# Output step of a gated Toeplitz layer: second half sorted by tile shape, the remaining channels in four quarters of the array

## The chip, the cores and the metric
One core of a Trainium2 chip runs the whole program. Times are device microseconds for one launch; a kernel's time is the median of its runs. The engines are TensorE (PE; its weight loads are listed as PEld), VectorE (DVE), ScalarE (ACT) and GpSimd (POOL). SyncE (SP) only issues transfers, and POOL issues some of them too.

## The reference
Four layers act one after the other on an image tensor `x` of 8 samples, 56 x 56 positions, 192 channels, all in fp32. Each is `x = x + layer(groupnorm(x))`. Layers 0 and 1 have this form:

```python
p = silu(x @ p_w.T + p_b)              # 192 -> 576 channels
q = silu(x @ q_w.T + q_b)
v = silu(x @ v_w.T + v_b)
o1 = toeplitz(q * v, a1)               # along the rows of the image
o2 = toeplitz(q * v, a2)               # along its columns
out = (p * (o1 + o2)) @ o_w.T + o_b    # 576 -> 192 channels
```

Layer 2 is a 7 x 7 depthwise convolution with an MLP, layer 3 a windowed attention. The change touches layers 0 and 1 only.

## The kernel before
**Stages of layers 0 and 1.** Samples are worked on in pairs (j and j + 4), and pairs in two groups of two (`j0` = 0 and 2). For each layer and group there are three stages. `tno_qv` (Q) computes `q * v` and writes it to DRAM. `tno_toeplitz` (TZ) multiplies it by Toeplitz matrices along rows and columns and writes the sum `o1 + o2` to the DRAM array `L_sum`, called `o` in the code. `tno_out` (O) reads the sum, computes `p`, gates, multiplies by `o_w` and writes the layer's result `y`.

**Weaving.** A planner (`weave`) runs one lane of stages and lets another generator emit a step whenever its share of the planned time is due. In order: TZ of layer 0, group 0 beside Q of group 1; TZ of layer 0, group 1 beside O of layer 0, group 0 (below: pass A) and Q of layer 1, group 0; TZ of layer 1, group 0 beside O of layer 0, group 1 (pass B) and Q of layer 1, group 1; TZ of layer 1, group 1 beside O of layer 1, group 0 (pass C); last, the convolution's first half beside O of layer 1, group 1 (pass D). PE, ACT, DVE and POOL keep the order in which the code emits their instructions during the Toeplitz stages. When a lane stage is 90% done, the rest of the Toeplitz steps is emitted and the first loads of the next O follow. So each pass's sums are complete before O loads them.

**Toeplitz stage.** Its 9 blocks hold 64 channels each. L405 multiplies in tiles of 56 rows x 32 columns of the array, 8 of them side by side. ACT copies (L412), DVE transposes (L423, L425), POOL adds the column direction (L427), and `store` issues four POOL transfers (L437) for each half of a block. `store` puts 128 channels into a *part* of `o`: parts 0 to 3 are the first 512 channels of the pair's first sample, 4 to 7 those of the second, and part 8 holds the remaining 64 channels of both samples, one on partitions 0 to 63, the other on 64 to 127 (`row + b // 2 * 64`). The ninth block is the one that goes to part 8.

**Output stage.** A tile is 224 positions of a pair; 14 tiles make a pair and 28 a pass. 576 channels are 4 x 128 + 64, and 192 are 128 + 64, so each product has pieces of four shapes. The moving operand always has 224 columns. `inner` computes `p` for the first 512 channels (L530: full array; L539: 64 rows x 128 columns, two at once), ACT applies Silu (L549) and POOL, in pass D DVE, multiplies into the sums (L556). `outer` works on two tiles at once: `now`, for which it makes the 64 remaining channels of `p` (`rem`; L565: 128 x 64, L567: 64 x 64), and `before`, the tile before it, whose output product it makes: 128 output channels from the remaining 64 inputs (L572: 64 x 128) and from the 512 (L575: full array), and 64 output channels (`po2`) from the 512 (L578: 128 x 64) and from the remaining 64 (L580: 64 x 64). `rem` and `po2` share one PSUM tile `P` of two banks with the 128-channel result: `po2` lies in the first bank, `rem` in the second. Then come Silu of `rem` (L584), its gate (L585), the residual (L588, L591), the store of `y` (L122, on POOL) and the statistics (L594). The sums' tile, three buffers deep, also takes the gated values and then `y`, so that a load of sums (L502, on SP) waits for a store of `y` from three tiles earlier.

Of the kernel before, what the change touches and what calls it, by code (L numbers as in the profile page):

```python
# [26 lines left out]
B, H, W, C = 8, 56, 56, 192  # L27
T = H * W
HALF = [slice(0, 64), slice(64, 128)]
TT = 448  # L30
NT = T // TT
D1 = 576
# [11 lines left out]
class Net:  # L44
# [320 lines left out]
    def tno_toeplitz(self, j0, mats, qv, o):  # L365

        nc, p = self.nc, self.tz
        PR = H // 2  # L370

        def load(n):
            blk, d = divmod(n, 2)
            q = p.tile([128, H, 128], F32, name="q", bufs=2)
            if d == 0:

                for half in range(2):
                    of = qv[2 * blk + half, :T].rearrange("(h w) e -> w h e", w=W)
                    nc.sync.dma_start(q[64 * half : 64 * half + W], of)  # L379
            else:  # L380
                of = qv[2 * blk : 2 * blk + 2].rearrange("n (h w) e -> (n h) (w e)", w=W)
                nc.sync.dma_start(q.rearrange("p i e -> p (i e)"), of)
            return q

        def matrices(n):

            blk, d = divmod(n, 2)
            row = 32 * self.TW
            at = mats[d].offset + 2 * blk * self.TG * row
            for k in range(4):  # L390
                of = bass.AP(mats[d].tensor, at + k, [[row, 2 * self.TG], [1, row]])
                nc.sync.dma_start(self.tms[n % 2][k:128:4], of)  # L392

        def along(n, q, ot, g):


            d, tm = n % 2, self.tms[n % 2]
            pt = self.bank2()
            for hf in range(2):
                for j in range(4):  # L400
                    c = 4 * g + j
                    at = c * self.TW + (28 if d else 24) * hf
                    for r in range(2):
                        rows = slice(64 * r, 64 * r + 56)
                        nc.tensor.matmul(  # L405
                            pt[32 * j : 32 * j + 32, r, hf * 224 : (hf + 1) * 224],
                            tm[rows, at : at + 32],
                            q[rows, :, 4 * c : 4 * c + 4],
                            start=True,
                            stop=True,  # L410
                        )
            nc.scalar.copy(  # L412
                view(ot, 4 * (g % 4), [[16, 2], [32, 112], [1, 4]]),
                view(pt, 0, [[512, 2], [4, 112], [1, 4]]),
            )

        def turned(d, ot, s, hf):


            of = ot[:, hf * 56 * 32 : (hf + 1) * 56 * 32]  # L420
            if d == 0:
                to = view(s, 55 - 24 * hf, [[W, 56], [-1, 32]])
                nc.vector.transpose(to, of.rearrange("p (i k) -> p i k", k=32))  # L423
            else:
                nc.vector.transpose(of, of)  # L425
                to = view(s, (55 - 28 * hf) * W, [[-W, 28], [1, 56]])
                nc.gpsimd.tensor_add(to, to, view(of, 0, [[1, 28], [32, 56]]))  # L427

        def store(blk, s, half):
            for b in range(4):  # L430
                part, row = divmod(blk * DC + 32 * half, 128)
                if part < 4:
                    part += b // 2 * 4
                else:
                    part, row = 8, row + b // 2 * 64
                to = o[j0 + b % 2, part, row : row + 32, :]
                nc.gpsimd.dma_start(to, s[b : 128 : 4])  # L437

        NS = 2 * (D1 // DC)
        loaded = []  # L440
        for n in range(2):
            loaded.append(load(n))
            matrices(n)
        yield 8.0

        work = []

        def behind():


            if work:
                d, ot, s, half, hf, blk = work.pop(0)
                turned(d, ot, s, hf)
                if d and hf:
                    store(blk, s, half)

        for n in range(NS):
            blk, d = divmod(n, 2)
            q = loaded.pop(0)
            if d == 0:  # L460
                ss = [p.tile([128, T], F32, name="s", bufs=2) for half in range(2)]
            for g in range(8):
                if g % 4 == 0:
                    ot = p.tile([128, 2 * 56 * 32], F32, name="ot", bufs=2)
                along(n, q, ot, g)
                if g % 4 == 3:
                    work += [(d, ot, ss[g // 4], g // 4, hf, blk) for hf in range(2)]
                if g % 2:
                    if g == 7 and n + 2 < NS:
                        loaded.append(load(n + 2))  # L470
                        matrices(n + 2)
                    yield 3.2
                    behind()
        while work:
            behind()

    def tno_out(self, L, j0, xs, gn, o, ys, gn_next, woven):
# [3 lines left out]
        nc, p, inp = self.nc, self.tp, self.inp  # L481
        N = 224
# [5 lines left out]
        pw = wo[:, : 2 * D1].rearrange("p (k c) -> p k c", k=2)  # L488
        ow = wo[:, 2 * D1 : 2 * D1 + 5 * C].rearrange("p (k c) -> p k c", k=5)
# [15 lines left out]
        def normalize(j, x):  # L505
            xn = p.tile([128, 3, N], F32, name="t4")
            for k in range(3):
                if woven:
                    nc.scalar.activation(  # L509
                        xn[:, k, :],  # L510
                        x[:, k, :],
                        AF.Identity,
                        bias=gn[:, j, k, 1:2],
                        scale=gn[:, j, k, 0:1],
                    )
                else:
                    nc.vector.tensor_scalar(
                        xn[:, k, :], x[:, k, :], gn[:, j, k, 0:1], gn[:, j, k, 1:2], ALU.mult, ALU.add
                    )
            return xn  # L520

        mm = nc.tensor.matmul
# [35 lines left out]
        def outer(now, before, after=None):  # L558

            P = self.bank2()  # L560
            po2, rem = P[:, 0, 256 : 256 + N], P[:, 1, 256 : 256 + N]
            if now:
                xn, s = now[5], now[3]
                for b in range(2):
                    mm(rem[HALF[b]], pw[:, 0, 512:D1], xn[:, b], start=True, stop=False)  # L565
                for b in range(2):
                    mm(rem[HALF[b]], pw[HALF[b], 1, 512:D1], xn[HALF[b], 2], start=False, stop=not before)  # L567
            if before:
                j, t, x, g, st, _ = before
                for b in range(2):  # L570
                    fresh = b == 0 or not now
                    mm(P[:, b, :N], ow[HALF[b], 4, 0:128], g[HALF[b], 8], start=fresh, stop=False)  # L572
                for c in range(4):
                    for b in range(2):
                        mm(P[:, b, :N], ow[:, c, 0:128], g[:, 4 * b + c], start=False, stop=c == 3 and b == 1)  # L575
                for c in range(4):
                    for b in range(2):
                        mm(po2[HALF[b]], ow[:, c, 128:C], g[:, 4 * b + c], start=False, stop=False)  # L578
                for e in range(2):
                    mm(po2[HALF[e]], ow[HALF[e], 4, 128:C], g[HALF[e], 8], start=False, stop=True)  # L580
            xn = normalize(*after) if after else None
            if now:
                pg = p.tile([128, N], F32, name="t1", bufs=1)
                nc.scalar.activation(pg, rem, AF.Silu, bias=pb[:, 4:5])  # L584
                gate.tensor_mul(s[:, 8], s[:, 8], pg)  # L585
            if before:
                y = g[:, 0:3]
                nc.vector.scalar_tensor_tensor(  # L588
                    y[:, 0:2], P[:, :, :N], ob[:, 0:1], x[:, 0:2], ALU.add, ALU.add
                )  # L590
                nc.vector.scalar_tensor_tensor(y[:, 2], po2, ob[:, 1:2], x[:, 2], ALU.add, ALU.add)  # L591
                self.store_pair(ys, j, slice(t * N, (t + 1) * N), y)
                for k in range(3):
                    nc.vector.bn_stats(st[:, k, t, :], y[:, k, :])  # L594
                if t == T // N - 1:
                    self.norms.append(self.pair_gn_finish(st, gn_next, j))
            return xn

        tiles = [(j, t) for j in (j0, j0 + 1) for t in range(T // N)]
        before = None  # L600
        x2 = load_x(*tiles[0])
        s = load_s(*tiles[0])
        if woven:
            yield None
            xn = normalize(j0, x2[:, :, :N])
        yield 0.0
        if not woven:
            xn = normalize(j0, x2[:, :, :N])
# [1037 lines left out]
```

## Time and profile before

| what | value |
| --- | --- |
| median of 3 runs | 5809.6 us (5804.27 to 5814.28) |
| profiled execution | 5811.1 us, its span 5809.3 us |
| PE busy | 5361.1 us, 92% of the span |
| POOL busy | 2207.7 us, 38% |
| pass A, B, C, D (us from the span's start) | 985 to 1415, 1790 to 2260, 2610 to 3235, 3235 to 3805 |
| granted TensorE clock | 0.957 of full speed over the span |

A line of the timeline has the start in us, the length in us, the engine, the line of the code, the operation, output and input tiles, for matmuls the rows * columns of the array in use and the shape, and how many instructions were merged (x16). In brackets stands how long the engine was idle before, and what ended that. An fp32 matmul appears as two records. A length runs to the modelled end of a pipelined matmul, so that start-to-start differences are the better measure of steps on PE.

### The profile page before, as it was taken

The numbers are of one execution on the slowest core, as the hardware profiler recorded it, in microseconds if no ns is written. First come the engines' busy times: TensorE is split into PE (matmuls) and PEld (weight loads), VectorE is DVE, ScalarE is ACT, GpSimd is POOL, SyncE is SP. The second block draws the span as 40 slices with busy tenths as digits, with TensorE's granted clock in tenths as the row PEclk, the third lists the DMA queues.
The fourth block names the chain that finished last, engine by engine and source line by source line (L and its number), as shares of the span: only waits on it lengthen the run. The fifth ranks groups of instructions, "written<-read, shape, count | busy, mean of one in ns | idle before, by whom it ended". The sixth has DMA issues, their size and how long they took to land.

```text
span 5809.3 us, 144273 instructions
## 1 busy us (share of the span) xinstructions
PE 5361.1 (92%) x64672; PEld 3889.9 (67%) x64672; DVE 2365.9 (41%) x3770; ACT 2269.1 (39%) x2990; POOL 2207.7 (38%) x1528
## 2 busy tenths in 40 slices
PE   6998888999999999998898889999999999989987
PEld 3776666777777777776676678855664445666765
DVE  6444444233553333552343322422113232555555
ACT  2434444444554444454444322242324333333332
POOL 2335565565565556565567100000001002333332
PEclk9999999999999999999999899999999999999998
DMA  8559997887886887978998556634444222434442
GB/s 277 137 150 263 274 293 217 261 255 225 246 262 197 254 245 236 251 218 239 296 307 266 175 200 223 212 127 162 145 149 117 67 67 54 85 90 93 88 95 48
DMA packets 1029771, 1098.79 MB, mean 189 GB/s; under 512 B 232769, under 2 KB 966977, under 8 KB 1013729
## 3 DMA queue, kind: packets, MB, share of 16 engines
q1 hardware_dynamic: 993568, 888.57, 55.6%
q0 software_dynamic: 35584, 200.99, 9.1%
q8 instruction: 509, 8.34, 0.6%
q14 instruction: 110, 0.89, 0.0%
HBM read 725.48 MB, written 363.94 MB: 188 GB/s over the span
## 4 chain that ended last, share of the span: by engine, by line
PE 59%; SPq 9%; DMA 9%; POOL 9%; DVE 7%; issue 4%; ACT 2%; POOLq 0%; DVEq 0%; ACTq 0%
PE bank L263 12%; PE bank L955 7%; PE bank L816 5%; PE bank L1035 4%; SPq L392 4%; PE bank L530 4%; POOL s L427 4%; PE bank L405 4%; PE bank L575 3%; DMA qv<-t 3%; SPq L379 3%; PE bank L1049 3%; DMA t<-L_sum 3%; PE bank L539 2%; PE bank L578 2%
## 5 line engine op out<-in xcount | busy, mean ns | idle before, releaser
L263 PE MATMUL bank<-wq,t 128*128 128x256 f32 (+4 forms) x7680 | 1293.7, 376 | 81.4 <-DVE t L272 41.6
L263 PEld LDWEIGHTS bank<-wq,t 128*128 128x128 f32 (+2 forms) x7680 | 1009.5, 191 | 359.5 <-issue 103.5
L272 DVE TENSOR_TENSOR t<-bank,wq 128x1024 f32<-128x1024 f32 (+3 forms) x480 | 517.7, 1112 | 774.0 <-PE bank L263 554.7
L304 POOL TENSOR_TENSOR t<-t 128x1024 f32<-128x1024 f32 (+2 forms) x288 | 519.5, 1818 | 650.0 <-ACT t L301 326.7
L412 ACT COPY ot<-bank 128x896 f32<-128x896 f32 x576 | 493.3, 914 | 622.4 <-PE bank L405 361.2
L427 POOL TENSOR_TENSOR s<-s,ot 128x1568 f32<-128x1568 f32 x144 | 618.9, 4303 | 64.8 <-DVE ot L425 64.1
L405 PE MATMUL bank<-q,tm 56*32 56x224 f32 x18432 | 523.0, 362 | 83.6 <-DMA tm<-L_tab 27.5
L301 ACT ACTIVATE t<-t 128x2048 f32<-128x2048 f32 (+2 forms) x288 | 421.9, 1488 | 398.2 <-DVE t L272 394.8
L405 PEld LDWEIGHTS bank<-q,tm 56*32 56x32 f32 x18432 | 352.6, 108 | 221.2 <-issue 117.5
L556 POOL TENSOR_TENSOR t<-t,t 128x896 f32<-128x896 f32 x168 | 347.4, 2086 | 358.7 <-DMA t<-L_sum 189.5
L588 DVE SCALAR_TENSOR_TENSOR t<-bank,wo,t 128x448 f32<-128x448 f32 x112 | 76.4, 682 | 890.0 <-ACT t L584 517.1
L530 PE MATMUL bank<-t,wo 128*128 128x224 f32 x1792 | 397.1, 378 | 44.4 <-ACT t L509 22.6
L955 PE MATMUL bank<-z,w 128*128 128x448 f32 (+1 forms) x1344 | 413.6, 555 | 2.0 <-ACT h L964 2.0
L549 ACT ACTIVATE t<-bank,wo 128x448 f32<-128x448 f32 x448 | 248.5, 635 | 407.2 <-PE bank L539 379.8
L530 PEld LDWEIGHTS bank<-t,wo 128*128 128x128 f32 x1792 | 352.5, 203 | 81.4 <-issue 28.2
L575 PE MATMUL bank<-t,wo 128*128 128x224 f32 x1792 | 378.6, 365 | 0.0
L127 POOL DMA_DIRECT2D x<-x x64 | 36.8, 575 | 862.4 <-DVE x L986 832.9
L575 PEld LDWEIGHTS bank<-t,wo 128*128 128x128 f32 x1792 | 337.7, 194 | 34.0 <-issue 32.3
L816 PEld LDWEIGHTS bank<-xt,cm 113*112 113x112 f32 x3072 | 315.0, 180 | 45.0 <-issue 37.4
L423 DVE STREAM_TRANSPOSE s<-ot 128x1792 f32<-128x1792 f32 x144 | 292.6, 2034 | 109.3 <-DMA L_sum<-s 63.9
L816 PE MATMUL bank<-xt,cm 113*112 113x108 f32 (+2 forms) x3072 | 326.2, 266 | 7.7 <-ACT h L964 4.5
L955 PEld LDWEIGHTS bank<-z,w 128*128 128x128 f32 (+1 forms) x1344 | 182.2, 189 | 205.8 <-issue 197.5
(149 smaller groups left out, 7004.3 us busy)
## 6 DMA issues: line engine op xcount, KB each, us to landing
q<-qv SPq DMA_DIRECT2D x36, 3584.0 KB
q<-qv SPq DMA_DIRECT2D x72, 1568.0 KB
L_sum<-s POOLq DMA_DIRECT2D x288, 392.0 KB, 7.2
t<-L_sum SPq DMA_DIRECT2D x112, 1008.0 KB
qv<-t SPq DMA_DIRECT2D x192, 512.0 KB
cm<-in_L_cm SPq DMA_DIRECT2D x96, 896.0 KB
tm<-L_tab SPq DMA_DIRECT2D x288, 240.0 KB
x<-t POOLq DMA_DIRECT2D x112, 336.0 KB, 7.0
```

The costliest lines, as they stand in the source:

```text
L263: nc.tensor.matmul(pp[:m, b, 256 * j : 256 * j + k], x[rows, j, 2 if part else b, s : s + m], w[rows, part, c0 + c : c0 + c + k],  start=p ...
L272: nc.vector.tensor_add(z[:m, c : c + k, :], view(pp[:m], 0, [[1, k], [256, 4]]), view(bias[:m], c0 + c, [[1, k], [0, 4]]),)
L301: nc.scalar.activation(z[:m, :n, :], z[:m, :n, :], AF.Silu)
L304: nc.gpsimd.tensor_mul(prod[:m, :k], half[:, :, 0], half[:, :, 1])
L405: nc.tensor.matmul(pt[32 * j : 32 * j + 32, r, hf * 224 : (hf + 1) * 224], tm[rows, at : at + 32], q[rows, :, 4 * c : 4 * c + 4], start=Tr ...
L412: nc.scalar.copy(view(ot, 4 * (g % 4), [[16, 2], [32, 112], [1, 4]]), view(pt, 0, [[512, 2], [4, 112], [1, 4]]),)
L427: nc.gpsimd.tensor_add(to, to, view(of, 0, [[1, 28], [32, 56]]))
L530: mm(gs[c // 2][:, b, c % 2 * 256 : c % 2 * 256 + N], pw[:, 0, 128 * c : 128 * c + 128], xn[:, b], start=c % 2 == 0, stop=False,)
L556: gate.tensor_mul(to, to, pg)
L575: mm(P[:, b, :N], ow[:, c, 0:128], g[:, 4 * b + c], start=False, stop=c == 3 and b == 1)
L816: nc.tensor.matmul(pc[:, 128 * e + 4 * m0 : 128 * e + 4 * m1], cm[:113, e, k, :], xt[:, m0 - 1 + k : m1 - 1 + k, c + e, :], start=n == 0 a ...
L955: nc.tensor.matmul(phs[c][:, s, :TT], w0[rows, part, at : at + 128], z[rows, Z[2 if part else s], :], start=part == flip, stop=part != flip,)
```

## The change
In `outer`, the matmuls are put in another order. First come up to four 64 x 64 products together: the two of `rem` from the 64-row piece and the two of `po2` from the remaining 64 channels. Then come the 128 x 64 products of `rem` and `po2`, then the 64 x 128, last the full-array products.

For the four 64 x 64 products to lie in four different quarters of the array, the two samples of the remaining channels change halves on every other tile (`turn` for `now`, `back` for `before`): on odd tiles `rem` is made with the samples' partitions exchanged, and the matmuls that read them follow. The sums have to come in the same arrangement, so `store` writes part 8 in two transfers per `b`, one for the even and one for the odd tiles of 224 positions, the latter to the other half of the partitions. The normalization of the next tile (`xn`) is emitted between the matmul groups and no longer after them.

```diff
-                else:
-                    part, row = 8, row + b // 2 * 64
-                to = o[j0 + b % 2, part, row : row + 32, :]
-                nc.gpsimd.dma_start(to, s[b : 128 : 4])
+                    to = o[j0 + b % 2, part + b // 2 * 4, row : row + 32, :]
+                    nc.gpsimd.dma_start(to, s[b : 128 : 4])
+                    continue
+                for turn in range(2):
+                    at = row + 64 * (b // 2 ^ turn)
+                    to, of = (
+                        ap.rearrange("p (t k n) -> p t k n", k=2, n=224)[:, :, turn]
+                        for ap in (o[j0 + b % 2, 8, at : at + 32, :], s[b : 128 : 4])
+                    )
+                    nc.gpsimd.dma_start(to, of)
...
+            turn = now[1] % 2 if now else 0
             if now:
                 xn, s = now[5], now[3]
-                for b in range(2):
-                    mm(rem[HALF[b]], pw[:, 0, 512:D1], xn[:, b], start=True, stop=False)
-                for b in range(2):
-                    mm(rem[HALF[b]], pw[HALF[b], 1, 512:D1], xn[HALF[b], 2], start=False, stop=not before)
             if before:
                 j, t, x, g, st, _ = before
+                back = t % 2
+            for b in range(2):
+                if now:
+                    r = HALF[b ^ turn]
+                    mm(rem[r], pw[HALF[b], 1, 512:D1], xn[HALF[b], 2], start=True, stop=False)
+                if before:
+                    r = HALF[b ^ back]
+                    mm(po2[HALF[b]], ow[r, 4, 128:C], g[r, 8], start=True, stop=False)
+            if now:
                 for b in range(2):
-                    fresh = b == 0 or not now
-                    mm(P[:, b, :N], ow[HALF[b], 4, 0:128], g[HALF[b], 8], start=fresh, stop=False)
-                for c in range(4):
-                    for b in range(2):
-                        mm(P[:, b, :N], ow[:, c, 0:128], g[:, 4 * b + c], start=False, stop=c == 3 and b == 1)
+                    mm(rem[HALF[b ^ turn]], pw[:, 0, 512:D1], xn[:, b], start=False, stop=not before)
+            xn = normalize(*after) if after else None
+            if before:
                 for c in range(4):
                     for b in range(2):
                         mm(po2[HALF[b]], ow[:, c, 128:C], g[:, 4 * b + c], start=False, stop=False)
-                for e in range(2):
-                    mm(po2[HALF[e]], ow[HALF[e], 4, 128:C], g[HALF[e], 8], start=False, stop=True)
-            xn = normalize(*after) if after else None
+                for b in range(2):
+                    r = HALF[b ^ back]
+                    mm(P[:, b, :N], ow[r, 4, 0:128], g[r, 8], start=b == 1 and not now, stop=False)
+                for c in range(4):
+                    for b in range(2):
+                        mm(P[:, b, :N], ow[:, c, 0:128], g[:, 4 * b + c], start=False, stop=c == 3)
```

More of the change, by code (lines that the diff above doesn't have):

```diff
@@ L432, in store @@
                 if part < 4:
-                    part += b // 2 * 4
-                else:
-                    part, row = 8, row + b // 2 * 64
-                to = o[j0 + b % 2, part, row : row + 32, :]
-                nc.gpsimd.dma_start(to, s[b : 128 : 4])
+                    to = o[j0 + b % 2, part + b // 2 * 4, row : row + 32, :]
[8 more added lines that the diff above has]
+                    nc.gpsimd.dma_start(to, of)
         NS = 2 * (D1 // DC)
```

## The prediction
> **What bounds the kernel now.** I read the page first for the engine shares, then a table of stretches for the four passes of the output step (A to D), then the timeline of single tiles, then the waits around the stores of a Toeplitz pass.
>
> ```profile
> PE 5361.1 (92%) x64672; PEld 3889.9 (67%) x64672; DVE 2365.9 (41%) x3770; ACT 2269.1 (39%) x2990; POOL 2207.7 (38%) x1528
> ```
> ```profile
> core 0: us, PE busy (x) PEld busy (x) DVE busy (x) ACT busy (x) POOL busy (x), PEclk, DMA share, GB/s
> 985.00:1415.00 430.00, 412.86 (x4672) 313.60 (x4671) 129.35 (x185) 182.61 (x302) 250.64 (x165) 0.98 0.87 252
> 1790.00:2260.00 470.00, 451.06 (x4933) 343.19 (x4932) 146.15 (x209) 201.07 (x327) 261.82 (x172) 0.97 0.86 246
> 2610.00:3235.00 625.00, 534.34 (x7148) 405.38 (x7145) 225.38 (x245) 259.08 (x396) 391.30 (x242) 0.92 0.92 272
> 3235.00:3805.00 570.00, 536.54 (x3989) 448.45 (x3989) 186.96 (x441) 148.03 (x256) 26.79 (x40) 0.95 0.57 194
> ```
> The rows are A, B, C and D. In A and B TensorE is 96% busy, in D 94%: PE is the first limit there. In C it is 85% busy with the DMA engines at 0.92; between 2700 and 3100 us they are at 1.0. There PE is not the limit.
>
> One tile of A, TensorE alone:
> ```profile
> 1266.85 1.74 PE L405 MATMUL bank<-q,tm 56*32 56x224 f32 x64
> 1268.53 0.60 PE L565 MATMUL bank<-t,wo 128*64 128x224 f32 x4
> 1269.06 0.59 PE L567 MATMUL bank<-t,wo 64*64 64x224 f32 x4
> 1269.58 0.65 PE L572 MATMUL bank<-t,wo 64*128 64x224 f32 x4
> 1270.16 3.29 PE L575 MATMUL bank<-t,wo 128*128 128x224 f32 x16
> 1273.39 1.73 PE L578 MATMUL bank<-t,wo 128*64 128x224 f32 x16
> 1275.05 0.59 PE L580 MATMUL bank<-t,wo 64*64 64x224 f32 x4
> ```
> "128*64" is the part of the array in use; each fp32 matmul is two records. Start to start, L578's 16 records take 1.66 us and L565's 4 take 0.53, so 12 records cost 1.13: 0.19 us per pair running together, and a fixed 0.15 us for entering a new shape (single records confirm it: 0.187 us apart in a shape, 0.279 across a change). L567 and L580 are two quarters of the array at 0.53 us for two steps; two quarters stand idle.
>
> **The change part by part.**
> 1. *Quarters.* L580's phase (0.53 us) disappears: its two products run beside the two of L567 in the other quarters. Saved 0.53 per tile, if all four run at once. The Trainium skill speaks against this: "TensorEngine Tiling (Array Packing)", Gotcha 1, says that different row tiles cannot access the same PSUM bank at the same time. Here each bank gets a result from the upper and one from the lower half of the rows. The row: L567 does exactly that already (both quarters write `rem` in one bank) and takes 0.53 for 4 records; one after another it would be 4 x 0.187 + 0.15 = 0.90. And L405 runs eight tiles at once: 64 records in 1.68 us, 8 steps. By the rule the phase would be two pairs and the saving 0.15 per tile; by the rows 0.53. I take the rows.
> 2. *Merging.* L565's 2 matmuls join L578's 8 (128*64): one entry less, 0.15.
> 3. *Ending in 128*128.* The outer part now ends with the full-array products, and the next inner part begins with such. Where they are adjacent an entry falls away. Nearest row: L530 after L816 (also full array) takes 3.14 us and waits 0.099 before its first record, after another shape 3.22 and 0.279; so 0.18. In the two kernels' instruction orders that holds for about 8 tiles in A, 8 in B, 4 in C and 27 in D (convolution matmuls are full-array too); elsewhere Toeplitz matmuls lie between.
> Sum on PE: 110 x 0.68 + 47 x 0.18 = 83 us, as 20 + 20 + 19 + 23.
> 4. *An earlier wait.* The quarters need `g[:, 8]` of the tile before, which L585 makes, at the head of the outer part; before, only L572 needed it, 1.05 us later. Behind the waiting matmul stand all of PE and, through it, L584 and L588. Normally L585 is done 3 to 8 us earlier. Not always:
> ```profile
> 1273.51 4.12 POOL L556 TENSOR_TENSOR t<-t,t 128x896 f32<-128x896 f32 x2 [10.21 <-DMA t<-L_sum]
> ...
> 1277.60 4.31 POOL L427 TENSOR_TENSOR s<-s,ot 128x1568 f32<-128x1568 f32 x1
> ...
> 1282.19 0.60 PE L565 MATMUL bank<-t,wo 128*64 128x224 f32 x4
> ```
> POOL waits for the sum's load, then does the gate, a Toeplitz add of 4.31, then L585 until 1282.54: 0.35 us after the outer part began. The load was released by a y store of three tiles earlier, so this loop is DMA and POOL time that the change does not shorten. Pairing L585's ends with L565's starts, A and B each have five such tiles (lead from -0.3 to -2.7 us). At each the lead shrinks by two tiles' saving, 1.35, and the 1.05 of `rem` work now runs after the wait: about 2.2 us lost, 11 per pass. A and B keep 9.5 each. In C I keep a third, 6 (PE idle 91 of 625 us, on tm loads and ACT copies, full DMA). In D the lead is mostly over 10 us; about a twentieth of the time PE waits on ACT and loads for the convolution, and with the first tiles I keep 18 of 23.
> 5. *Stores.* The last block's 8 stores of a Toeplitz pass become 16, each 224 runs of 896 B instead of 32 of 12.5 KB; same bytes. POOL's issue takes 0.53 us for L437 (32 runs), 0.576 for L127 (128), 0.81 for L122 (384): about 0.66 for 224. Per pass 16 x 0.66 - 8 x 0.53 = 6.3 us of POOL. Bounds: 4.2 at 0.53, 8.7 at 0.81. Two tails expose it. After the first pass POOL's stores stand ahead of the L304 that L272 and PE wait for:
> ```profile
> 972.04 2.09 POOL L437 DMA_DIRECT2D L_sum<-s  x4 [0.29 <-POOL s L427]
> 974.14 3.03 POOL L304 TENSOR_TENSOR t<-t 128x1024 f32<-128x1024 f32 x2
> ...
> 977.81 3.23 PE L263 MATMUL bank<-wq,t 128*128 128x128 f32 x16 [10.50 <-DVE t L272]
> ```
> After the last pass both groups of stores stand ahead of L585:
> ```profile
> 3185.53 2.14 POOL L437 DMA_DIRECT2D L_sum<-s  x4 [0.29 <-POOL s L427]
> ...
> 3188.42 1.12 PE L572 MATMUL bank<-t,wo 64*128 64x224 f32 x4 [11.21 <-POOL t L585]
> ```
> Cost 2 x 6.3, and about 1.5 more because `rem` work that filled the start of the second gap comes after it. The other two tails I cost at nothing: one unbroken PE run of 58.5 us (L263 from 1763.4 and from 2592.2) covers them; without that cover 6.3 each. Landing: these stores took 2.6 to 16 us before and L122's small-run stores 2.8 to 17.3 (medians 7.2 and 7.0), so I add nothing for the small runs; the first sums are used 25 us after their load was issued at 976.92, which covers POOL's delay.
> 6. *No cost.* ACT, DVE and SP run the same instructions; against before one pair changes places on each (L584 on ACT, L556 on DVE, a qv store and an x load on SP). The normalization moved up in the text keeps its place on its engine. SP reads the sums with the same shape.
>
> Sum: 9.5 + 9.5 + 6 + 18 - 12.6 - 1.5 = 29. The profiled execution took 5811.1 us (span 5809.3), 1.5 above the median of the runs, 5809.6. From it 5782; against the median 5781.
>
> **The rivals.**
> - *The waits move along with PE* (25%). If the POOL and DMA times in A to C follow the earlier PE, as where a Toeplitz add was released by a PE result, the loss at the ten tight tiles falls to the reordering, about 0.4 each: A and B keep 16 each, C 12, D 21, stores 8: 57 us, 5752. For it: most tiles are apart by exactly the sum of PE's steps (12.0, 13.7, 15.3). Against: the tight tiles root in DMA waits.
> - *Four quarters do not run at once, or A to C gain nothing* (15%). By the rule above the PE sum falls by 110 x 0.37 = 41; with the same losses and the stores nothing is left, 5800 to 5815. The same time comes if the load loop takes all of A, B and C: 18 - 14 = 4. Against: L567 and L405.
> - *The small stores cost more than the matmuls give* (20%), the slower side. The 29 stand after 12.6 of stores, so 42 without. With two tails exposed it turns at (42 / 2 + 4.2) / 16 = 1.6 us per store; with all four exposed at (42 / 4 + 4.2) / 16 = 0.92. The dearest store issue of the trace, 2016 runs in one qv store, takes 1.16 us; at that price and four tails 4 x (18.6 - 4.2) = 58 are lost, 16 more than won: 5826. Against: 384 runs cost 0.81. For: 16 stores of small runs in a row have no row here, and the sum's first load must wait for them to land.
> - *The likeliest case* above: 40%.
>
> **How the numbers follow.** About 0.2% (12 us) is what a measurement of this kernel can tell from no change. Faster by more: nearly all of the first rival and of the likeliest case, and little of the others: 0.65. Within: the second rival's middle and the edges: 0.16. Slower: the third rival and the tail of the second: 0.19. The range goes from the first rival's 5752, with a few us below it, to 5816, half way into the third.
>
> **What would show it.** Right: the second phase of an outer part with 8 records of 64*64 in about 0.54 us; no 64*64 phase at its end; 20 records of 128*64 in about 2.04; L530 right after the full-array products in 3.14 or less; outer parts of 6.38 instead of 7.05. POOL's last-block stores at 0.6 to 0.7 us each; the gap before 977 grown from 10.5 to about 17 and the one before 3188 from 11.2 to about 19. PE's waits for L585 grown from a few us to over ten in A and in B. D shorter by some 18 us, A and B by half of that. Wrong: 64*64 phases of 0.9 us; stores of 1 us and more, or a first output tile that waits for its sums; A and B as long as before.

## The result, and the profile after
The median went from 5811.0 us (12 runs beside it) to 5805.7 us: ratio 0.9992 [0.9983, 1.0002]. A gain of 29 us was forecast; 5 us came, which this measurement cannot tell from nothing. The profiled execution took 5813.5 us (span 5811.7; before: 5811.1 and 5809.3).

The engine shares of the changed kernel, from the page:
```profile
PE 5303.4 (91%) x64672; PEld 3883.4 (67%) x64672; DVE 2364.6 (41%) x3770; ACT 2267.7 (39%) x2990; POOL 2227.7 (38%) x1560
```
PE is 57.7 us less busy than before, at the same number of matmuls, and the span is 2.4 us longer. So PE's work did shrink, and waits filled what it left. With every busy stretch weighted by the clock granted in it, PE's busy time fell from 5166 to 5096 us, by 70: some 12 us more than 57.7, given back because more of the work ran at half clock. POOL is 20 us busier, with 32 records more: the 64 store issues of the last block in place of 32.

The table of stretches for passes A to D, at the windows used before:
```profile
core 0: us, PE busy (x) PEld busy (x) DVE busy (x) ACT busy (x) POOL busy (x), PEclk, DMA share, GB/s
985.00:1415.00 430.00, 403.79 (x4690) 315.52 (x4692) 131.64 (x186) 186.78 (x309) 250.56 (x165) 0.97 0.87 255
1790.00:2260.00 470.00, 437.70 (x4913) 341.38 (x4919) 145.81 (x208) 194.13 (x318) 270.24 (x182) 0.96 0.85 243
2610.00:3235.00 625.00, 515.90 (x7135) 399.95 (x7134) 221.03 (x235) 262.24 (x398) 403.00 (x254) 0.91 0.92 270
3235.00:3805.00 570.00, 525.55 (x4042) 455.13 (x4042) 189.09 (x447) 148.42 (x257) 32.20 (x44) 0.95 0.59 200
```
PE's busy time fell by 9 to 18 us in every row. Windows of fixed times do not move with the kernel, so lengths are better taken between a pass's own ends (start of the first matmul of L530, now L535, to the start of the last store of `y`):

| us | before | after | change | forecast |
|---|---|---|---|---|
| start of the program to A | 994.5 | 1003.0 | +8.5 | +6.3 |
| pass A | 425.8 | 419.3 | -6.5 | -9.5 |
| A to B | 401.6 | 410.0 | +8.4 | 0 |
| pass B | 424.8 | 421.7 | -3.1 | -9.5 |
| B to C | 404.1 | 411.7 | +7.6 | 0 |
| pass C, with the last tail | 579.8 | 587.3 | +7.5 | +1.8 |
| pass D | 570.0 | 551.4 | -18.6 | -18 |

D came as forecast, A and B together gave half of it, and three stretches that hold stores at a tail (the end of a Toeplitz pass, where its last block is stored) became 8 us longer each, where one had been charged. (Each column is one execution. The first stretch runs from 992.6 to 1007.4 us in the six kernels below and above that store alike in it, so its +8.5 is within the scatter. The two stretches between passes are steadier: they take 410.0 to 412.8 us in the three kernels in which POOL issues 16 stores for the last block, and 400.9 to 405.7 in the eleven others of this document.)

One tile of A, PE alone. It begins with the new second phase, four of whose eight records are shown, one to a row:
```profile
1299.35 0.40 PE L576 MATMUL bank<-t,wo 64*64 64x224 f32 x1
1299.36 0.40 PE L579 MATMUL bank<-t,wo 64*64 64x224 f32 x1
1299.36 0.40 PE L576 MATMUL bank<-t,wo 64*64 64x224 f32 x1
1299.37 0.40 PE L579 MATMUL bank<-t,wo 64*64 64x224 f32 x1
...
1299.89 0.60 PE L582 MATMUL bank<-t,wo 128*64 128x224 f32 x4
1300.32 1.68 PE L587 MATMUL bank<-t,wo 128*64 128x224 f32 x16
1301.93 0.65 PE L590 MATMUL bank<-t,wo 64*128 64x224 f32 x4
1302.51 3.29 PE L593 MATMUL bank<-t,wo 128*128 128x224 f32 x16
1305.64 3.19 PE L535 MATMUL bank<-t,wo 128*128 128x224 f32 x16
1308.76 1.78 PE L544 MATMUL bank<-t,wo 64*128 64x224 f32 x16
```
Four matmuls start within 0.02 us; the phase lasts from 1299.35 to 1299.89, 0.54 us for 8 records. L582 and L587 together take 2.04 us, L535 after L593 3.12. All three are the forecast's figures: an undisturbed outer part takes 6.38 us in place of 7.05; where a full-array product follows it takes 6.29, and L535 there takes 3.12 in place of 3.22.

The last block's store issues:
```profile
L442 POOL DMA_DIRECT2D L_sum<-s x64: 611/623/687, 963.5 to 3208.5; - x64
```
A median of 623 ns against the 660 of the forecast: per pass 16 x 0.62 - 8 x 0.53 = 5.7 us more on POOL.

The tail of the second Toeplitz pass, POOL, DVE and PE. First the kernel before, then the changed one:
```profile
1763.33 58.60 PE L263 MATMUL bank<-wq,t 128*128 128x256 f32 x368
...
1785.68 2.17 POOL L437 DMA_DIRECT2D L_sum<-s  x4 [0.29 <-POOL s L427]
1787.87 6.04 POOL L304 TENSOR_TENSOR t<-t 128x256 f32<-128x256 f32 x4
...
1788.64 0.69 DVE L272 TENSOR_TENSOR t<-bank,wq 128x512 f32<-128x512 f32 x1 [5.16 <-POOL t L304]
```
```profile
1791.94 4.93 POOL L442 DMA_DIRECT2D L_sum<-s  x8 [0.30 <-POOL s L427]
1796.89 6.02 POOL L304 TENSOR_TENSOR t<-t 128x256 f32<-128x256 f32 x4
...
1797.66 0.69 DVE L272 TENSOR_TENSOR t<-bank,wq 128x512 f32<-128x512 f32 x1 [10.69 <-POOL t L304]
...
1798.41 33.95 PE L263 MATMUL bank<-wq,t 128*128 128x256 f32 x200 [3.81 <-DVE t L272]
```
The forecast took the unbroken PE run of 58.6 us as cover. Under it DVE was already waiting 5.16 us for L304, which stands behind the stores in POOL's order. With the stores longer, that wait is 10.69 us; the buffers that L304 frees come too late for L272, PSUM is not emptied, and PE stops for 3.81 us in the middle of the "unbroken" run. The window just behind, before and after (columns as in the table of stretches):
```profile
1798.00:1805.00 7.00, 7.00 (x40) 5.66 (x40) 2.83 (x3) 3.51 (x6) 3.08 (x2) 1.00 0.90 266
```
```profile
1798.00:1805.00 7.00, 6.59 (x24) 4.77 (x24) 3.40 (x4) 2.54 (x2) 5.50 (x4) 0.55 0.63 200
```
The granted clock is 0.55 for 7 us after that stop: busy as before, with 24 records done in place of 40. That is an estimated 7 x 0.45 = 3 us more, and with the stop about 7 of the 8.4 us. The third tail has the same stop:
```profile
2632.25 33.47 PE L263 MATMUL bank<-wq,t 128*128 128x256 f32 x200 [4.40 <-DVE t L272]
```

At the first tail and at the last the stops grew about as forecast (to 17 and 19), from 10.5 to 16.0 and from 11.2 to 18.1 us:
```profile
985.64 3.23 PE L263 MATMUL bank<-wq,t 128*128 128x128 f32 x16 [15.96 <-DVE t L272]
```
```profile
3204.23 4.90 POOL L442 DMA_DIRECT2D L_sum<-s  x8 [0.30 <-POOL s L427]
3209.16 0.67 POOL L597 TENSOR_TENSOR t<-t,t 128x224 f32<-128x224 f32 x1
...
3209.88 0.63 PE L579 MATMUL bank<-t,wo 64*64 64x224 f32 x1 [18.08 <-POOL t L597]
```

### The profile page after: what moved, and what is told of

The parts are those of the page before. It is cut to its first block, busy times and chain, and to the rows that moved or that the text cites. A ratio compares the mean times of both kernels' runs of the same rounds, so it can differ in the third digit from the quotient of the medians.

```text
span 5811.7 us, 144299 instructions
## 1 busy us (share of the span) xinstructions
PE 5303.4 (91%) x64672; PEld 3883.4 (67%) x64672; DVE 2364.6 (41%) x3770; ACT 2267.7 (39%) x2990; POOL 2227.7 (38%) x1560
## 4 chain that ended last, share of the span: by engine, by line
PE 51%; SPq 8%; POOL 8%; DMA 7%; DVE 5%; issue 4%; ACT 2%; POOLq 0%; DVEq 0%; ACTq 0%
PE bank L263 7%; PE bank L967 6%; PE bank L828 5%; SPq L392 5%; PE bank L1047 4%; PE bank L535 3%; PE bank L593 3%; POOL s L427 3%; SPq L379 3%; PE bank L405 3%; PE bank L1061 3%; DMA t<-L_sum 2%; PE bank L1241 2%; PE bank L544 2%; POOL t L561 2%
## 5 line engine op out<-in xcount | busy, mean ns | idle before, releaser
L272 DVE TENSOR_TENSOR t<-bank,wq 128x1024 f32<-128x1024 f32 (+3 forms) x480 | 517.9, 1112 | 785.6 <-PE bank L263 556.4
L304 POOL TENSOR_TENSOR t<-t 128x1024 f32<-128x1024 f32 (+2 forms) x288 | 518.9, 1816 | 651.6 <-ACT t L301 345.6
L405 PE MATMUL bank<-q,tm 56*32 56x224 f32 x18432 | 526.9, 365 | 90.1 <-DMA tm<-L_tab 34.5
L405 PEld LDWEIGHTS bank<-q,tm 56*32 56x32 f32 x18432 | 353.4, 109 | 226.8 <-issue 119.8
L561 POOL TENSOR_TENSOR t<-t,t 128x896 f32<-128x896 f32 x168 | 347.5, 2087 | 371.1 <-DMA t<-L_sum 184.5
L535 PE MATMUL bank<-t,wo 128*128 128x224 f32 x1792 | 394.9, 375 | 63.4 <-ACT t L514 28.7
L535 PEld LDWEIGHTS bank<-t,wo 128*128 128x128 f32 x1792 | 351.4, 202 | 96.3 <-ACT ot L412 36.6
L554 ACT ACTIVATE t<-bank,wo 128x448 f32<-128x448 f32 x448 | 248.3, 635 | 396.6 <-PE bank L544 353.9
L593 PE MATMUL bank<-t,wo 128*128 128x224 f32 x1792 | 369.0, 359 | 0.0
L593 PEld LDWEIGHTS bank<-t,wo 128*128 128x128 f32 x1792 | 330.0, 190 | 32.0 <-issue 32.0
```

The source lines that it names most:

```text
L272: nc.vector.tensor_add(z[:m, c : c + k, :], view(pp[:m], 0, [[1, k], [256, 4]]), view(bias[:m], c0 + c, [[1, k], [0, 4]]),)
L304: nc.gpsimd.tensor_mul(prod[:m, :k], half[:, :, 0], half[:, :, 1])
L405: nc.tensor.matmul(pt[32 * j : 32 * j + 32, r, hf * 224 : (hf + 1) * 224], tm[rows, at : at + 32], q[rows, :, 4 * c : 4 * c + 4], start=Tr ...
L535: mm(gs[c // 2][:, b, c % 2 * 256 : c % 2 * 256 + N], pw[:, 0, 128 * c : 128 * c + 128], xn[:, b], start=c % 2 == 0, stop=False,)
L561: gate.tensor_mul(to, to, pg)
```

## The experiments
Three theories were to be told apart. *Stores:* the 16 issues of a tail cost time at all four tails, more than was charged. *Head wait:* the quarters at the head of the outer part, which need the gate of the tile before (L597), cost more than was charged. *Load loop:* in A and B the sum's load and POOL set the pace, so PE's saving is worth little whatever the order. Each has 4 to 13 runs; ratios are to runs of the kernel before measured beside them, and the change in us is that ratio applied to its 5811 us. An interval is 0.17 to 0.33% wide, 10 to 19 us, so differences of a few us between two rows mean nothing.

| kernel | median us | ratio [95%] | change us |
|---|---|---|---|
| e1 before, stores split | 5823.4 | 1.0033 [1.0020, 1.0046] | +19 |
| e2 after, stores as before | 5778.0 | 0.9957 [0.9943, 0.9972] | -25 |
| e3 after, exchange made by the load | 5767.9 | 0.9936 [0.9922, 0.9949] | -37 |
| e4 after, quarters second | 5786.5 | 0.9962 [0.9950, 0.9975] | -22 |
| e5 both e3 and e4 | 5758.6 | 0.9922 [0.9908, 0.9936] | -45 |
| e6 sorted, two pairs at the head | 5799.9 | 0.9993 [0.9985, 1.0002] | -4 |
| e7 sorted, two pairs second | 5767.2 | 0.9943 [0.9930, 0.9955] | -33 |
| e9 after, split stores issued by SP | 5759.3 | 0.9925 [0.9913, 0.9938] | -44 |
| e10 e4, split stores issued by SP | 5745.5 | 0.9903 [0.9888, 0.9918] | -56 |
| e11 e5, all stores of sums by SP | 5787.4 | 0.9965 [0.9952, 0.9978] | -20 |
| e12 before, last block's stores by SP | 5792.4 | 0.9979 [0.9969, 0.9990] | -12 |
| e13 e5, last block's stores by SP | 5745.2 | 0.9906 [0.9890, 0.9923] | -55 |

**e1: the split alone**, in the kernel before, without the exchange.
```diff
-    part, row = 8, row + b // 2 * 64
-to = o[j0 + b % 2, part, row : row + 32, :]
-nc.gpsimd.dma_start(to, s[b : 128 : 4])
+for turn in range(2):
+    at = row + 64 * (b // 2)
+    ...    # runs of 224, as in the change
+    nc.gpsimd.dma_start(to, of)
```


> The kernel before with one thing of the change: the last block's stores are split in two by even and odd tiles (16 instead of 8 per Toeplitz pass), without exchanging the samples. Theory 1 (all four tails are exposed, and every gap that they make on TensorE is followed by a stretch at half clock): about 8 us per tail, 25 to 32 us slower than before, 5836 to 5843. Theory 2 (only POOL's extra time at two tails, as forecast; the rest of the gain was lost in waits inside the passes): 6 to 13 us slower, 5817 to 5824.

Measured +19 us, between the two theories' ranges. The three stretches with a first, second and third tail grew by 4.4, 9.8 and 8.6 us, and pass C by 5.2. The matmuls are untouched, so this is the stores' price at four tails, and the cover of the two middle ones is gone without any saving on PE. That all four tails count is theory 1's part; its price per tail was too high.

**e2: the change without the split.**
```diff
-for turn in range(2):
-    at = row + 64 * (b // 2 ^ turn)
-    ...
+    part, row = 8, row + b // 2 * 64
+nc.gpsimd.dma_start(o[j0 + b % 2, part, row : row + 32, :], s[b : 128 : 4])
```


> The changed kernel with the stores of the kernel before (8 per pass). The exchange of samples on odd tiles is therefore missing in the sums of the last 64 channels. Theory 1: the whole cost of the stores comes back, about 30 us: 5772 to 5780. Theory 2: only 6 to 13 us come back, 5793 to 5800.

Measured -25 us, 20 us better than the change, again between the ranges. (The exchange is left out of the sums here, so this kernel shows a time and is no usable version.) The stretches to B and C are 403.0 and 403.5 us, against 410.0 and 411.7 with the split and 401.6 and 404.1 before. The loss there is the stores'.

**e3: the exchange made by the load.** Stores as before; for odd tiles SP reads the last 64 channels' halves crosswise.
```diff
+nc.sync.dma_start(s[:, :8], of[:, :8])
+for b in range(2):
+    nc.sync.dma_start(s[HALF[b], 8], of[HALF[1 - b], 8])
```


> The changed kernel, stores as before, and the exchange made at the load instead: on odd tiles the sums come in three transfers on SP (parts 0 to 7, and the two halves of part 8 crossed), 112 more transfers on SP in all. Theory 1, with the loads hidden: as e2, 5772 to 5782. Rival: the load of sums is the tight loop in A and B, and two more issues of 0.36 us on SP and small transfers make it longer: 5785 to 5800.

Measured -37 us. This kernel computes what the change computes, with all its matmuls in their places, and is 32 us faster: two more DMAs per odd tile on SP cost nothing that shows. The gap to e2 (12 us) is not settled, as the two intervals overlap.

**e4: the quarters second.** The 128*64 products go first, the quarters after them.
```diff
+for b in range(2):
+    mm(rem[HALF[b ^ turn]], pw[:, 0, 512:D1], xn[:, b], start=True, stop=False)
+for c in range(4):
+    for b in range(2):
+        mm(po2[HALF[b]], ow[:, c, 128:C], g[:, 4 * b + c], start=c == 0, stop=False)
 for b in range(2):
     ...    # the four quarters, start=False
```


> The changed kernel with the 128*64 products first and the four quarters after them, same number of shape changes; the gated last 64 channels are needed 2 us later. If the earlier wait at the head costs the tight tiles about 2 us each (ten in A and B, a few in C): 10 to 22 us faster than the changed kernel, 5784 to 5796. If POOL and the load loop set those tiles and the wait only moves to the second place: no change from the changed kernel, 5802 to 5809.

Measured -22 us, 17 us better than the change: 10.0 in C, 6.4 in D, 1.2 and 2.7 in A and B (single executions). So the head wait cost the changed kernel 17 us, of the size that was charged, but for the most part in other places. PE's waits of the changed kernel in the window 2640 to 3260, with the total, the number and the longest:
```profile
PE bank L405 <- DMA tm<-L_tab: 32.0, 6, 9.0
PE bank L579 <- POOL t L597: 29.6, 3, 18.1
PE bank L535 <- ACT ot L412: 24.3, 4, 8.2
```
and of e4 in the same window (the quarters' line is now L588):
```profile
PE bank L588 <- POOL t L599: 16.1, 1, 16.1
```
The three waits of 29.6 us are the last tail and the two tiles behind it. There POOL starts the convolution's buffers, and in the changed kernel both long memsets stand ahead of the gate:
```profile
3214.78 12.50 POOL L763 MEMSET xt<- 17x7424 f32 x2
3227.36 0.66 POOL L597 TENSOR_TENSOR t<-t,t 128x224 f32<-128x224 f32 x1
```
In the kernel before and in e4 POOL's written order is one memset, the gate, the other memset. With the quarters at the head (in e2, e3 and e6 too) it is memset, memset, gate. PE waits 4.50 us for this gate and 7.06 for the next; in e4 0.28 and 5.38, for L561. Against the kernel before this is no loss, as it has one wait of 11.61 us there; it is what e4 wins over the change.

**e5: e3 and e4 together.**

> Both remedies together: the four quarters second (e4) and the exchange at the load, with the stores of the kernel before (e3). If store cost and head wait are two separate losses, they add up: 31 + 17 us faster than the changed kernel, about 50 us faster than before, ratio 0.9905 to 0.992. If both only relieve the same POOL waits at the tails, the sum is little more than e3 alone: ratio 0.993 to 0.9945.

Measured -45 us, ratio 0.9922, between the two forecasts. The two gains add up only in part: e3's 32 and e4's 17 would have made 54 less than before. Passes A and B are 416.1 and 419.4 us, 9.7 and 5.4 shorter than before; PE's steps promise 20 each.

**e6 and e7: sorted, but with two pairs in place of four quarters** (stores as before, no exchange), at the head or second.
```diff
-turn = now[1] % 2 if now else 0
+turn = 0
-back = t % 2
+back = 0
```


> The sorted order alone: no exchange of samples, so the four 64*64 products lie on the two diagonal quarters and run as two pairs, at the head of the outer part; stores and loads as before. TensorE's sum is 83 - 110 x 0.37 = 42 us. Theory: D gives about 13 us, A to C lose what they win at the head wait (as in e2): 5 to 20 us faster than before, ratio 0.9965 to 0.999, and 5 to 20 us slower than e2. If four quarters are worth nothing (A to D bound elsewhere): as e2, 0.9957.

> As e6, with the 128*64 products first and the two pairs of 64*64 after them, so without the head wait and without any extra transfer. Theory: e6 and about 15 us more, as e4 against the changed kernel: 20 to 30 us faster than before, ratio 0.995 to 0.9965; e5 is then better by the quarters, 10 us in D and what A to C let through, 10 to 30 us in all. If the quarters are hidden in A to C, e5 and this differ by 10 us only.

At the head nothing is won that can be told from no change (5 to 20 us were expected), second 33 us (20 to 30 were); here the head wait is worth 29. Two phases of e6, then the next:
```profile
1303.96 0.60 PE L571 MATMUL bank<-t,wo 64*64 64x224 f32 x4
1304.39 0.55 PE L574 MATMUL bank<-t,wo 64*64 64x224 f32 x4
1304.87 0.60 PE L577 MATMUL bank<-t,wo 128*64 128x224 f32 x4
```
Start to start 0.43 and 0.48: 0.91 us for what the four quarters do in 0.54. That pair phase is what the change's quarters would have taken if they ran two by two. The quarters' own gain is e6 to e2, 21 us, and e7 to e5, 12 us (the latter with e3's loads).

**e9: the change, with the 16 stores issued by SP.**
```diff
-nc.gpsimd.dma_start(to, of)
+nc.sync.dma_start(to, of)
```


> The changed kernel with the 16 last-block stores of each pass issued on SP instead of POOL; the matmuls and the small runs stay. If POOL's issue time is the cost, it goes away altogether (before, 8 issues took 4.3 us): as e2 or better, ratio 0.993 to 0.996. If the small runs and their landing are the cost, or SP's queue holds up the loads of sums behind stores that wait for POOL: as the changed kernel or slower, 0.9985 to 1.003.

Measured -44 us, more than was expected: 39 us from one word. This takes more than the split off POOL, since the eight issues of the kernel before are gone too; e2, which has those, is 19 us slower.

**e12: that word in the kernel before**, for its eight last-block stores.
```diff
-nc.gpsimd.dma_start(to, s[b : 128 : 4])
+(nc.gpsimd if part < 8 else nc.sync).dma_start(to, s[b : 128 : 4])
```


> The kernel before with one edit: the 8 last-block stores of each Toeplitz pass are issued on SP instead of POOL, in one piece as before. If POOL's issue time of those stores lies on the path to the end at all four tails, its 4.3 us per pass come off: 4 x 4.3 = 17 us faster than before, ratio 0.9965 to 0.998. If only two tails are exposed: 8 us, 0.998 to 0.9995. If the tails have other reasons, no change.

Measured -12 us, between 17 for four exposed tails and 8 for two. The first tail, by its PE row:
```profile
972.84 3.23 PE L263 MATMUL bank<-wq,t 128*128 128x128 f32 x16 [5.60 <-DVE t L272]
```
5.60 us of waiting, in place of 10.50 before and 15.96 after. The stretches to B and C do not shrink (405.6 and 404.3 us): the cover there was just enough for eight issues, and not for sixteen.

**e10: quarters second and the split stores on SP.**

> The changed kernel with the four quarters second (e4) and the split stores of the last block on SP (as e9). If the head wait and POOL's issue time are two losses that add up: e9 and 17 us more, about 60 us faster than before, ratio 0.989 to 0.9905. If they overlap at the tails: little more than e9 or e5, 0.9915 to 0.993.

**e13: e5 with the last block's stores on SP**, unsplit.

> The quarters second and the exchange at the load (e5), with the 8 unsplit last-block stores of each pass on SP. Stores as in e12, so 10 to 15 us more than e5: 55 to 62 us faster than before, ratio 0.989 to 0.991. It stands against e10, which has 16 small-run stores on SP and no extra loads: if small runs or extra loads cost anything off POOL, the two differ; if issue time on POOL is all, both are the same within 0.15%.

-56 and -55 us, the same, both as expected. These are the fastest versions, about 1% below the kernel before and 0.9% below the change. e10 has the small runs in its stores, e13 the extra loads, so off POOL neither costs anything that shows; the price was POOL's issue time. Second place for the quarters is worth 12 us here (e9 to e10) and 8 in e3 to e5, where the intervals overlap: less than the 17 and 29 above.

**e11: e5 with every store of sums on SP.**
```diff
-nc.gpsimd.dma_start(to, s[b : 128 : 4])
+nc.sync.dma_start(to, s[b : 128 : 4])
```


> The fifth kernel (quarters second, exchange at the load) with all 72 stores of sums of each Toeplitz pass on SP. POOL is freed of 288 issues of 0.53 us, 153 us in all. If POOL's time in A to C is what holds back the matmuls' gain there: 20 to 50 us more than e5, ratio 0.983 to 0.9885. Rival: SP's queue is in order, so a store that waits for POOL's add holds the loads of sums, tm and q behind it: as e5 or slower, 0.992 to 1.0.

Measured -20 us, 25 us worse than e5, as the rival in its expectation had it. SP issues in order, and a store that waits for POOL's add holds the loads behind it. SP's own waits, and PE's for the Toeplitz matrices (26.2 us over 6 waits in e5):
```profile
SPq L437 <- POOL s L427: 337.7, 59, 14.9
```
```profile
PE bank L405 <- DMA tm<-L_tab: 63.7, 14, 10.3
```
For this kernel, then, the queue to choose is the one whose next work is not urgent: SP for the last block, where no load of the same pass follows, POOL for the others.

A version with four buffers for the sums, which would have tested the load loop directly, was not run.

## Why the prediction was wrong
**Quarters, merging, ending in 128*128 (steps 1 to 3): right.** 0.54, 2.04 and 3.12 us were forecast and measured. The rule that different row tiles cannot access one PSUM bank at the same time ("TensorEngine Tiling (Array Packing)", Gotcha 1, in the Trainium skill) does not hold for these four quarters: four starts within 0.02 us, and e6's pairs show what one after another costs, 0.91. Choosing the row over the rule was right. (Of the two rows that the prediction gave, only L567 bears on this: in L405 each half of the rows writes a bank of its own.)

**Stores (step 5): this step failed, in its sentence "The other two tails I cost at nothing".** The size per store was right (0.62 for 0.66) and so were the two open tails. But the cover was read from PE alone. PE's run was unbroken because the engine behind it, DVE, had enough slack; DVE's row in the trace of before, waiting 5.16 us for POOL, said that POOL was already late there. The price the prediction named for the lost cover was 6.3 us each; the stretches grew by 8.4 and 7.6, the rest being PE at half clock behind the stop. In all 14 us were charged; the stores cost 19 us by e1, 20 by e2 and 32 by e3.

**The earlier wait (step 4): right in mechanism, wrong in size and in part in place.** Charged were 11 us each in A and B, and nothing named at the end of C. In A, PE's waits for the gate grew from 3.1 us (three, for L585) to 6.8 in five places, where "over ten" was forecast. A cost that was not forecast comes with each: the wait falls between the quarters, so that the first runs alone and the other three after it.
```profile
1312.15 0.59 PE L576 MATMUL bank<-t,wo 64*64 64x224 f32 x2
1313.75 0.40 PE L579 MATMUL bank<-t,wo 64*64 64x224 f32 x1 [1.01 <-POOL t L597]
```
Such an outer part takes 6.97 us without its wait, and not 6.38: the quarters win next to nothing there. Together some 3.7 + 5 x 0.59 = 7 us in A, where 11 were charged. What e4 takes back is 1.2 and 2.7 us in A and B, but 10.0 in C and 6.4 in D. Item 6 counted the pairs of instructions that change places on ACT, DVE and SP and passed over POOL, where a memset of 6.28 us had moved ahead of the gate that the quarters wait for.

**A and B kept 6.5 and 3.1 us, not 9.5.** In A, between its own ends, PE's busy time fell by 14.7 us, from 407.2 to 392.5, and its idle time rose from 18.6 to 26.8 us:
```profile
PE bank L579 <- POOL t L597: 6.8, 5, 2.0
```
In e4 that wait is gone, but waits for ACT's L554 (5.5 us, against 0.4) and L514 (11.5, against 10.3) stand in its place. Behind them POOL still waits for the sums:
```profile
1111.13 4.11 POOL L561 TENSOR_TENSOR t<-t,t 128x896 f32<-128x896 f32 x2 [16.27 <-DMA t<-L_sum]
```
Such waits come to 86 us in A before, 76 after, 92 in e4. No version brought A below 416 us. That the load loop sets this floor fits the runs and is argued, not shown.

**C: the 6 us were not won.** The waits at its end grew from 22.8 us (two, for L585) to 29.6 (three, for L597), which is all but 1 us of the pass's +7.5; the growth is that of the wait behind the stores, 11.2 to 18.1. The rest of C, with the DMA engines at 1.0 between 2700 and 3100 us before and after, gave back what PE saved: waits for `tm` loads 32.0 us against 24.9, for ACT's copies 24.3 against 14.7.

**D: right**, -18.6 for -18. Here POOL and the DMA engines are free enough (0.59), and PE's saving is the pass's.

Of the rivals, the one on the slower side (small stores that cost more than the matmuls give) came nearest, by its own turning point for four exposed tails, though not by its price: with 42 us from the matmuls it would have turned at 0.92 us per store; with the 25 us that e2 shows, the same sum turns at (25 / 4 + 4.2) / 16 = 0.65, close to the 0.62 measured (e3's 37 would make it 0.84). Against the forecast's -29, the two middle tails account for 16 us, C for 6, A and B for 9, and the first stretch for 2; D gives 1 back. That makes 32 us by the table, against 24 by the medians; the difference lies within the scatter of single executions.

## What to carry to other kernels
Before calling a cost covered by a long busy run, read the engines that feed that run: a wait of theirs on the engine that gets the extra work is a sign that the cover's slack is being used up (here DVE waited 5.16 us, and 5.7 us more on POOL broke the run). When a phase is sorted for the array, put last what needs another engine's newest result; here the order within the sort was worth 8 to 29 us over four pairs of kernels, about as much as the packing's 12 and 21. And look at who issues a store: issued by SP in place of POOL, which also computes, the same sixteen stores gained 39 us in the change and 34 in e4; all 72 of a pass on SP lost 25, since urgent loads stood behind them.

## What the hardware showed
A short stop can cost more than itself. In the kernel before, PE waits 1.13 us, after two stops of 0.6 to 0.7 us in the 7 us ahead of it, and then runs at about half clock:
```profile
2200.84 0.74 PE L572 MATMUL bank<-t,wo 64*128 64x224 f32 x4 [1.13 <-POOL t L585]
2201.51 4.84 PE L575 MATMUL bank<-t,wo 128*128 128x224 f32 x16
```
```profile
2201.00:2205.00 4.00, 4.00 (x14) 3.34 (x15) 0.00 (x0) 1.83 (x4) 3.98 (x2) 0.57 0.88 341
```
The 16 records take 4.84 us in place of 3.29, and the granted clock of the window around them (second fence) is 0.57. After the 3.81 us stop of the second tail the same happened for 7 us. It does not follow every stop: behind another of 1.13 us, shortly before, the clock stayed at 1.00.
```profile
2182.78 0.60 PE L565 MATMUL bank<-t,wo 128*64 128x224 f32 x4 [1.13 <-ACT t L549]
```
```profile
2182.00:2186.00 4.00, 2.88 (x18) 1.87 (x19) 0.00 (x0) 3.11 (x6) 3.98 (x4) 1.00 0.28 97
```
Part of what an exposed wait cost here is this; what decides it no run here shows.

The size of a store's runs had been counted as a risk of its own. 224 runs of 896 B in place of 32 of 12.5 KB showed only in POOL's issue time (0.62 us for 0.53); issued by SP they cost nothing that shows (e10 and e13 are equal).
